# Layer 1's scan units ordered by pair of states instead of by channel group

## The chip, the core and the metric

The kernel runs on one core of a Trainium2 chip. The metric is the device time of one launch in microseconds. A core has several engines, each with an in-order queue of its own: TensorE (PE in the profile; PEld is its weight load), VectorE (DVE), ScalarE (ACT), GpSimd (POOL) and SyncE (SP, which here only issues DMAs). They share SBUF, 128 partitions of on-chip memory; PSUM, which TensorE writes its products to, is a second one; layer 1 lays it out as two tiles of 128 x 1024 f32 and four banks of 128 x 512. GpSimd does not touch PSUM in this kernel. An engine waits for another through semaphores, which a framework sets wherever one instruction needs what another wrote, or wants to overwrite what another still reads.

## What is computed

Two layers on an image of 64 x 64 positions with 96 channels. Each is a group norm, then a selective state-space scan, then a residual sum. The change lies in layer 1 alone, which scans the 4096 positions in one direction with 192 inner channels and 16 states:

```python
xz = jnp.einsum('blc,ec->ble', u, W_in)
xs, z = jnp.split(xz, 2, axis=-1)
xc = jax.nn.silu(causal_conv3(xs) + conv_b)
dbc = jnp.einsum('bld,ed->ble', xc, W_x)          # dt (6), B (16), C (16)
delta = jax.nn.softplus(jnp.einsum('blr,dr->bld', dt, W_dt) + b_dt)
dA = jnp.exp(delta[..., None] * A)
dBu = delta[..., None] * Bm[:, :, None, :] * xc[..., None]
def step(h, inp):
    dA_t, dBu_t, C_t = inp
    h = dA_t * h + dBu_t
    y = jnp.einsum('bdn,bn->bd', h, C_t)
    return (h, y)
...
y = (y + xc * D) * jax.nn.silu(z)
return jnp.einsum('bld,cd->blc', y, W_out)
```

(`causal_conv3` stands here for the sum over three shifted copies.) There are 192 x 16 scans over 4096 positions.

## The kernel before

The positions are cut into four **chunks** of 1024. The 192 channels form three **groups** of 64, and the 16 states eight **pairs** (n, n + 8). A **unit** is one group with one pair: 64 channels x 2 states fill the 128 partitions, 1024 positions lie along the free axis. A chunk has 24 units, the layer 96. Before the change unit i of a chunk is group i // 8 with pair i % 8, so eight units of a group run one after the other.

What one unit s needs, with the functions of class `Layer1`:

- `decay(s)`: ScalarE computes dA = exp(A dt), where dt is the group's row block, doubled onto both halves of the partitions (the **dup** tiles, made by `front_dup` with SP's DMAs, once for each group and chunk, for dt and for w = dt times u).
- B spread over the partitions. For most units `spread(s)` lets TensorE do it: a product of a 0/1 matrix (`pick`) with B, where B has been split into three bf16 parts that sum to its f32 value (`front_b`: ScalarE rounds, GpSimd subtracts). It lands in a PSUM tile `f`, and VectorE multiplies it by w in place (first half of `scan`). For the 20 units listed in `POOL_UNITS`, `load` fetches B from DRAM by DMA into a tile `B`, GpSimd multiplies it by w (`pool_f`), and dA goes to a PSUM tile `f`. Units 0 to 3 of the layer (`WHOLE`) take B unsplit in f32.
- `scan(s)`: VectorE's TENSOR_TENSOR_SCAN gives h from dA, w B and the last column of the chunk before. `keep_last` lets ScalarE keep that column.
- `times_c(s)`: GpSimd multiplies C by h, in place in the tile `C`, which `load(s)` has fetched by DMA, two DMAs of 256 KB for every unit.
- `fold(s)`, three units later (`LAG`): TensorE sums the two halves and the pairs into the group's PSUM bank `y0`, `y1` or `y2`, after `skip` has put D times u there. When a group's eight units are folded, `gate` multiplies by silu(z) on VectorE, into a tile `v`, and `back` makes the output of the chunk.

The `f` tiles come from one ring of two PSUM tiles of 128 x 1024; `y0`, `y1`, `y2` and `misc` hold one bank each. All other products of a chunk (convolution, projections, dt, z, output) go through `misc`, one at a time, with an eviction by ScalarE behind each.

The order is written out by hand. `Ordered` (from line 373; its `call` records every instruction, so that the profile gives line 389 for nearly all of layer 1) chains the instructions of each engine in the order in which the program names them. `run` goes through the units s; in each step it takes one piece of the generator `between` (the next chunk's projections and convolution, the output of the chunk before), then loads, spread, decays, one piece of `soft` (the next chunk's softplus: ScalarE's functions, two VectorE steps in `soft_vector`, w on GpSimd), the scan of unit s, C times h of unit s - 1, the fold of unit s - 3, and `hold`, products with a zero matrix that only keep TensorE at work. `start` prepares chunk 0 before the first unit: convolution, projections, and the softplus of the first two thirds of its columns (groups 0 and 1; dt and u hold 1536 columns, 512 in each part, and part 2 is group 2's). `end` closes the last chunk.

Of the kernel before, what the change touches and what calls it, by code (L numbers as in the profile page):

```python
# [39 lines left out]
WHOLE = 4  # L40

# [3 lines left out]
POOL_UNITS = ((5, 11, 15, 19, 23), (4, 8, 12, 16, 21), (4, 8, 12, 16, 21), (4, 8, 12, 16, 20))  # L45
# [1236 lines left out]
class Layer1:  # L1282
# [6 lines left out]
    def __init__(self, nc, tc, st, k, lay, w_in, conv_w, x1, stats, bc_dram, out, g):  # L1289
# [4 lines left out]
            for n, b in (  # L1294
                ("fix", 1), ("xn", 2), ("uz", 2), ("sp", 1), ("dt", 2), ("dup", 2), ("dbl", 1),
                ("parts", 2), ("split", 1), ("B", 1), ("C", 4 + LAG), ("dA", 3), ("h", 3), ("v", 1), ("oc", 1),
                ("ob", 2),
# [53 lines left out]
    def steps(self, matmuls):  # L1351

        for i, (args, kw) in enumerate(matmuls):
            self.nc.tensor.matmul(*args, **kw)
            if i % 2 or i == len(matmuls) - 1:
                yield
# [45 lines left out]
    def front_u(self, c):  # L1402
        of, self.at = self.chunks[c], c
        of["u"] = u = self.tile("uz", [P, CW], "u")
        for q in range(3):
            ps = self.misc(c, [P, NB], f"pc{q}")
            yield from self.steps(self.product(ps, q, self.conv_taps(of["xn"])))
            self.nc.scalar.activation(
                u[:, self.part(q)], ps, AF.Identity, bias=self.vec(CB, q)
            )  # L1410
# [27 lines left out]

    def front_dbl(self, c):
# [3 lines left out]
        for hf in range(2):  # L1443
# [3 lines left out]
            self.write_bc(c, hf)  # L1447

# [10 lines left out]
    def front_w(self, c, cols, engine):  # L1459
        of = self.chunks[c]  # L1460
        if "w" not in of:
            self.at = c
            of["w"] = self.tile("dt", [P, CW], "w")
        for col in cols:
            engine.tensor_mul(of["w"][:, col], of["dt"][:, col], of["u"][:, col])

    def front_dup(self, c, g, parts=(slice(0, CH),)):
# [4 lines left out]
        if not dup:  # L1472
            for name in ("dt", "w"):
                dup[name] = self.tile("dup", [P, CH], f"{name}1")
# [12 lines left out]
    def of_unit(self, name, s):  # L1487
        c, i = divmod(s, UNIT)
        return self.chunks[c]["dup"][i // PAIRS][name]

    def front_b(self, c, halves=False):

        nc, of = self.nc, self.chunks[c]
        dbl = of["dbl"]
        self.at = c
        of["B"] = parts = self.tile("parts", [B_ROWS, CH], "parts", BF16)
        rest = self.tile("split", [B_ROWS, CH], "rest")
        mid = self.tile("split", [B_ROWS, CH], "mid", BF16)
        copy = nc.gpsimd.tensor_copy if halves else nc.scalar.copy
        for col in (self.part(0), self.part(1)) if halves else (slice(0, CH),):  # L1500
            nc.scalar.copy(parts[:, col], dbl[0:B_ROWS, col])
            if not halves:
                yield
            nc.gpsimd.tensor_sub(rest[:, col], dbl[0:B_ROWS, col], parts[:, col])
            if not halves:
                yield
            copy(mid[64:96, col], rest[64:96, col])
            copy(parts[32:64, col], rest[32:64, col])
            if not halves:
                yield  # L1510
            nc.gpsimd.tensor_sub(parts[64:96, col], rest[64:96, col], mid[64:96, col])
            yield


    def on_pool(self, s):


        c, i = divmod(s, UNIT)
        return c < NSC and i in POOL_UNITS[c]

    def load(self, s):
        self.at, of = s, self.units[s]
        c, i = divmod(s, UNIT)
        for part, name in enumerate("BC"):
            if part or self.on_pool(s):
                of[name] = self.tile(name, [P, CH], name)
                load_states(
                    self.nc, of[name], self.bc_dram[part], 0, UNITS[1][i % PAIRS], c
                )

    def decay(self, s):
        self.at = s
        i = s % UNIT
        pool = "f" if self.on_pool(s) else "dA"
        self.units[s]["dA"] = da = self.tile(pool, [P, CH], pool)
        self.nc.scalar.activation(
# [3 lines left out]
    def spread(self, s):  # L1540
        self.at = s
        c, i = divmod(s, UNIT)
        self.units[s]["f"] = f = self.tile("f", [P, CH], "f")
        for hf in range(2):
            if s < WHOLE:
                pick, of = self.k["first"][:, i, :], "dbl"
            else:
                pick, of = self.k["pick"][:, i % PAIRS, :], "B"
            self.nc.tensor.matmul(
                f[:, self.part(hf)], pick, self.chunks[c][of][0:B_ROWS, self.part(hf)],  # L1550
# [3 lines left out]
    def scan(self, s):  # L1554
        self.at, of = s, self.units[s]
        c, i = divmod(s, UNIT)
        if not self.on_pool(s):
            self.nc.vector.tensor_mul(of["f"], of["f"], self.of_unit("w", s))
        of["h"] = self.tile("h", [P, CH], "h")
        self.nc.vector.tensor_tensor_scan(  # L1560
            of["h"], of["dA"], of["f"], self.last[:, i : i + 1] if c else 0.0, ALU.mult, ALU.add
# [7 lines left out]
    def keep_last(self, s):  # L1569
        i = s % UNIT  # L1570
        self.nc.scalar.copy(self.last[:, i : i + 1], self.units[s]["h"][:, CH - 1 : CH])

    def times_c(self, s):
        of = self.units[s]
        self.nc.gpsimd.tensor_mul(of["C"], of["C"], of["h"])
# [16 lines left out]
    def skips(self, c):  # L1592
        for g in range(1, GROUPS):
            self.skip(c, g)

    def fold(self, s):
        nc, k, terms = self.nc, self.k, self.units[s]["C"]
        c, i = divmod(s, UNIT)
        g, n = divmod(i, PAIRS)
        if i == 0:  # L1600
# [7 lines left out]

# [450 lines left out]
```

## Time and profile before

| | us |
|---|---|
| three runs | 576.94, 579.02, 594.4; median 579.02 |
| profiled execution, its own time | 575.46 |
| its span | 573.6 |
| layer 0 and the start of layer 1, to the first unit's multiply on VectorE | 189.9 |
| the 96 units, to the end of the last scan | 367.7 |
| from there to the end of the span | 16.0 |

Busy time in the span: TensorE 488.0 us, VectorE 469.2, GpSimd 345.8, ScalarE 329.2. In the stretch from 200 to 560 us it is about 309, 331, 299 and 202 of 360 us, added up from the busy time in windows.

How to read the profile: rows name an instruction as output<-inputs by the tiles' names, with partitions x elements, the number of such instructions, their busy time and the mean duration of one in ns, then the idle time of the engine just before them and what ended most of it. The timeline has start, duration, engine and instruction, and in brackets the idle time before it and what released it. A group's eight units run in a cadence of one multiply and one scan each on VectorE, or one scan alone where GpSimd does the multiply. PEclk is the clock that TensorE was granted; over the execution its mean is 0.897. SPq is the DMA queue that SP issues to.

### The profile page before, as it was taken

How to read it: one execution, taken by the hardware profiler on the slowest of the kernel's cores; microseconds unless marked ns; L12 is line 12 of the kernel's file. 1: busy time of each engine (PE TensorE's matmuls, PEld its weight loads, DVE VectorE, ACT ScalarE, POOL GpSimd, SP SyncE). 2: the span in 40 equal slices, each digit the busy share in tenths (PEclk: the TensorE clock that was granted, in tenths of full speed). 3: DMA queues.
4: the chain of work that ended last, by engine and by line, in shares of the span. 5: the costliest groups of instructions: out<-in, count | busy, mean ns of one | idle time of the engine just before them, and what ended most of it. 6: DMA issues, size and time to landing. Idle time of an engine off the chain costs nothing.

```text
span 573.6 us, 5312 instructions
## 1 busy us (share of the span) xinstructions
PE 488.0 (85%) x1493; PEld 168.3 (29%) x1493; DVE 469.2 (82%) x447; ACT 329.2 (57%) x486; POOL 345.8 (60%) x206
## 2 busy tenths in 40 slices
PE   4999899988899596987798988979958768989794
PEld 3544354447632221221222222212212111222121
DVE  6897989248614599989989979999979989899981
ACT  5448993479454695677575684664584545243300
POOL 7080000015210496968987978788877888797960
PEclk9999999999997697988989978969987775997998
DMA  5103800000006954895989994997995897999901
GB/s 169 25 9 82 269 2 0 0 1 1 24 4 157 237 152 123 196 236 128 212 200 247 225 226 125 236 215 182 231 233 150 207 207 186 231 229 230 233 19 34
DMA packets 35241, 84.24 MB, mean 147 GB/s; under 512 B 13313, under 2 KB 14589, under 8 KB 34947
## 3 DMA queue, kind: packets, MB, share of 16 engines
q1 hardware_dynamic: 33922, 82.29, 60.1%
q10 hardware_dynamic: 1280, 1.52, 0.8%
q8 instruction: 14, 0.23, 0.2%
q14 instruction: 25, 0.20, 0.1%
HBM read 68.99 MB, written 2.25 MB: 124 GB/s over the span
## 4 chain that ended last, share of the span: by engine, by line
PE 34%; DVE 27%; ACT 18%; DMA 8%; POOL 5%; issue 4%; SPq 3%; DVEq 0%; POOLq 0%; ACTq 0%
DVE h L389 17%; PE y L389 8%; PE pc L389 7%; DVE f L389 5%; ACT q L389 3%; DMA C<-bc_dram 3%; PE f L389 3%; SPq L389 3%; ACT L389 3%; PE po L389 3%; DMA B<-bc_dram 2%; ACT f L389 2%; PE pz L389 2%; PE pw L389 2%; DMA dt<-dt 2%
## 5 line engine op out<-in xcount | busy, mean ns | idle before, releaser
L389 POOL TENSOR_TENSOR C<-C,h 128x1024 f32<-128x1024 f32 x96 | 227.7, 2388 | 36.9 <-DVE h L389 17.1
L389 DVE TENSOR_TENSOR_SCAN h<-dA,last,f 128x1024 f32<-128x1024 f32 x57 | 133.8, 2347 | 8.4 <-POOL C L389 0.7
L389 PE MATMUL y<-C,both 128*64 128x512 f32 x384 | 120.6, 714 | 1.9 <-POOL C L389 1.9
L389 DVE TENSOR_TENSOR f<-f,w 128x1024 f32<-128x1024 f32 x76 | 92.2, 1213 | 17.4 <-PE f L389 11.8
L389 ACT ACTIVATE dA<-dt,A 128x1024 f32<-128x1024 f32 x76 | 86.3, 1142 | 4.3 <-DMA dt<-dt 2.7
L389 PE MATMUL f<-parts,pick 96*128 96x512 bf16 x144 | 50.6, 438 | 26.2 <-DVE h L389 23.4
L389 PE MATMUL pc<-pad,cw 96*128 96x512 f32 (+1 forms) x144 | 57.3, 555 | 3.3 <-ACT v L389 3.3
L389 POOL TENSOR_TENSOR B<-B,w 128x1024 f32<-128x1024 f32 x20 | 47.6, 2378 | 19.8 <-DMA B<-bc_dram 6.1
L389 ACT COPY last<-h 128x1 f32<-128x1 f32 x72 | 13.5, 188 | 71.8 <-DVE h L389 71.8
L389 PE MATMUL y<-within,zeros 128*128 128x512 f32 x82 | 48.6, 693 | 0.0
L389 DVE TENSOR_TENSOR_SCAN h<-dA,f 128x1024 f32<-128x1024 f32 x19 | 43.5, 2287 | 2.4
L389 PE MATMUL pc<-xn,cw 96*64 96x512 f32 (+1 forms) x84 | 34.4, 679 | 12.4 <-ACT dt L389 6.5
L389 ACT ACTIVATE f<-dt,A 128x1024 f32<-128x1024 f32 x20 | 22.3, 1115 | 34.7 <-DVE h L389 26.2
L389 ACT ACT_TABLE_LOAD x28 | 35.9, 1283 | 8.6 <-DMA dt<-dt 6.5
L389 PEld LDWEIGHTS y<-C,both 128*64 128x64 f32 x384 | 22.1, 149 | 56.3 <-issue 42.5
L389 PEld LDWEIGHTS pc<-pad,cw 96*128 96x128 f32 x144 | 26.9, 189 | 33.3 <-issue 25.8
L389 DVE TENSOR_TENSOR_SCAN h<-f,last,B 128x1024 f32<-128x1024 f32 x15 | 34.9, 2329 | 1.4 <-POOL B L389 1.4
L389 PEld LDWEIGHTS <-pick 96*128 96x128 bf16 x144 | 10.3, 102 | 87.4 <-DVE h L389 50.5
L389 POOL TENSOR_TENSOR rest<-dbl,parts 96x1024 f32<-96x1024 f32 (+1 forms) x5 | 8.7, 1744 | 32.5 <-ACT parts L389 32.4
L389 POOL TENSOR_SCALAR ln_small<-ln_small 128x4 f32<-128x4 f32 x2 | 0.5, 235 | 42.5 <-DVE ln_small L389 42.5
L389 PEld LDWEIGHTS y<-within,zeros 128*128 128x128 f32 x82 | 14.3, 209 | 36.5 <-issue 36.5
L389 POOL MEMSET wda<- 128x4 f32 (+3 forms) x8 | 1.0, 119 | 37.5 <-ACT wda L389 37.5
(214 smaller groups left out, 736.1 us busy)
## 6 DMA issues: line engine op xcount, KB each, us to landing
C<-bc_dram SPq DMA_DIRECT2D x192, 256.0 KB, 5.2
B<-bc_dram SPq DMA_DIRECT2D x40, 256.0 KB, 4.7
dt<-dt SPq DMA_DIRECT2D x14, 256.0 KB, 4.8
w<-w SPq DMA_DIRECT2D x14, 256.0 KB, 7.6
dt<-dt SPq DMA_DIRECT2D x20, 128.0 KB, 4.7
w<-w SPq DMA_DIRECT2D x20, 128.0 KB, 5.3
wB<-rows_dram SPq DMA_DIRECT2D x1, 1472.0 KB
wC<-rows_dram SPq DMA_DIRECT2D x1, 1472.0 KB
```

Source lines behind the costliest of these rows:

```text
L389: ins = it(*args, **kw)
```

## The change

Unit i of a chunk is now pair i // 3 with group i % 3, so three units in a row share B and C.

- B is spread once for three units (`spread(s)` where s % 3 is 0), into `self.b`. The second and third unit (and unit 0 of the layer) multiply it by w into another `f` tile, `self.f`, which both use. The first unit of every three has its w B from GpSimd: 31 units instead of 20.
- C is loaded once for three units, B once for each that GpSimd multiplies. h tiles are 16 columns longer, the scan writes them from column 16 on, and `times_c` writes its product into the same tile from column 0 on, so that C stays.
- The split of B into bf16 parts is done by TensorE and ScalarE: ScalarE rounds from PSUM, and `less` lets TensorE subtract what has been rounded, by a product of the f32 rows with the identity and one of the bf16 parts with -1 entries (`k["less"]`).
- All three groups' dup tiles must be there from a chunk's first units on. In `start` the softplus of the third part is done with the other two, and the first part of chunk 1's convolution is made there as well. The dup tiles of groups 0 and 1 are filled in turn, part by part.
- The gates of a chunk come in the first steps of the next one, in place in `sz`; those of the last chunk come after the last scan. `hold`'s places change (37 of them, before 41), and so do the buffers of the tile pools.

The core of the diff:

```diff
-                ("fix", 1), ("xn", 2), ("uz", 2), ("sp", 1), ("dt", 2), ("dup", 2), ("dbl", 1),
-                ("parts", 2), ("split", 1), ("B", 1), ("C", 4 + LAG), ("dA", 3), ("h", 3), ("v", 1), ("oc", 1),
-                ("ob", 2),
+                ("fix", 1), ("xn", 2), ("uz", 2), ("sp", 1), ("dt", 1), ("dup", 2), ("dbl", 1),
+                ("parts", 2), ("B", 2), ("C", 3), ("dA", 3), ("h", 3 + LAG), ("oc", 1), ("ob", 2),
...
+    def less(self, i, c, hf, ps):
+        of, col = self.chunks[c], self.part(hf)
+        self.nc.tensor.matmul(
+            ps, self.k["ident"][0:B_ROWS, 0:B_ROWS], of["dbl"][0:B_ROWS, col],
+            start=True, stop=False,
+        )
+        self.nc.tensor.matmul(ps, self.k["less"][:, i, :], of["B"][:, col], start=False, stop=True)
+
+    def split(self, c, hf, ps, bank):
+        of, col = self.chunks[c], self.part(hf)
+        if "B" not in of:
+            self.at = c
+            of["B"] = self.tile("parts", [B_ROWS, CH], "parts", BF16)
+        for i, rows in enumerate((slice(0, B_ROWS), slice(0, 64), slice(32, 64))):
+            self.nc.scalar.copy(of["B"][rows, col], ps[rows, :])
+            if i < 2:
+                ps = bank(f"less{i}_{hf}")
+                yield lambda ps=ps, i=i: self.less(i, c, hf, ps)
...
     def on_pool(self, s):
-        c, i = divmod(s, UNIT)
-        return c < NSC and i in POOL_UNITS[c]
+        return s % GROUPS == 0 and 0 < s < NSC * UNIT
...
     def scan(self, s):
         if not self.on_pool(s):
-            self.nc.vector.tensor_mul(of["f"], of["f"], self.of_unit("w", s))
-        of["h"] = self.tile("h", [P, CH], "h")
+            if i % GROUPS == (1 if s > GROUPS else 0):
+                self.f = self.tile("f", [P, CH], "f")
+            of["f"] = self.f
+            self.nc.vector.tensor_mul(of["f"], self.b, self.of_unit("w", s))
+        of["h"] = self.tile("h", [P, CH + SHIFT], "h")
         self.nc.vector.tensor_tensor_scan(
-            of["h"], of["dA"], of["f"], self.last[:, i : i + 1] if c else 0.0, ALU.mult, ALU.add
+            of["h"][:, SHIFT:], of["dA"], of["f"], self.last[:, i : i + 1] if c else 0.0,
+            ALU.mult, ALU.add,
         )
...
     def times_c(self, s):
-        of = self.units[s]
-        self.nc.gpsimd.tensor_mul(of["C"], of["C"], of["h"])
+        h = self.units[s]["h"]
+        self.nc.gpsimd.tensor_mul(h[:, 0:CH], h[:, SHIFT:], self.units[s - s % GROUPS]["C"])
...
     def start(self):
...
-        for p in range(2):
+        pc1 = bank("y2", [P, NB], "pc1")
+        do(self.product(pc1, 0, self.conv_taps(self.chunks[1]["xn"])))
+        self.at = 1
+        self.chunks[1]["u"] = self.tile("uz", [P, CW], "u")
+        for p in range(3):
             col = self.part(p)
             nc.scalar.activation(sq[:, col], pv[p], AF.Abs, bias=self.vec(DTB, p))
             soft_scalar(nc, self.k, sq[:, col], acc[:, col], sq[:, col])
             nc.vector.tensor_scalar(dt[:, col], pv[p], self.vec(DTB, p), 0.0, ALU.add, ALU.max)
-        for s in range(3):
-            self.load(s)
-        for p in range(2):
+        self.load(1, 0)
+        self.load(0, 3)
+        self.load(1, 3)
+        for p in range(3):
             col = self.part(p)
             soft_vector(nc, dt[:, col], acc[:, col], sq[:, col])
-            self.front_w(0, (col,), nc.vector)
-            self.front_dup(0, 0, (col,))
+            self.front_w(0, col, nc.vector)
+            if p < 2:
+                for g in range(2):
+                    self.front_dup(0, g, (col,))
+        self.front_dup(0, 2)
         self.spread(0)
-        self.spread(1)
+        for s in range(2):
+            self.decay(s)
+        nc.scalar.activation(
+            self.chunks[1]["u"][:, self.part(0)], pc1, AF.Identity, bias=self.vec(CB, 0)
+        )
+        parts = [
+            self.split(0, hf, pd[hf], lambda name, y=f"y{hf}": bank(y, [B_ROWS, NB], name))
+            for hf in range(2)
+        ]
+        for _ in range(3):
+            for later in [next(part, None) for part in parts]:
+                if later:
+                    later()
         pz = [bank(f"y{g}", [P, NB], f"pz{g}") for g in range(GROUPS)]
         for g in range(GROUPS):
             do(self.z_product(pz[g], g, xn))
-        for s in range(2):
-            self.decay(s)
-        nc.scalar.activation(dt[:, self.part(2)], pv[2], AF.Identity, bias=self.vec(DTB, 2))
-        for _ in self.front_b(0, halves=True):
-            pass
...
     def run(self):
...
-            if 1 <= s < WHOLE:
-                self.spread(s + 1)
+            self.late = None
+            if 0 < c and 1 <= i <= GROUPS:
+                self.gate(c - 1, i - 1)
+            if s % GROUPS == 0 and 0 < s < n:
+                self.spread(s)
             if s < n:
                 next(work, None)
-            if s + 3 < n:
-                self.load(s + 3)
-            if WHOLE <= s < n - 1 and not self.on_pool(s + 1):
-                self.spread(s + 1)
+            if s % GROUPS == 1:
+                self.load(0, s + 5)
+            if s % GROUPS == 2:
+                self.load(1, s + 4)
             if 0 < s <= n - UNIT:
                 self.keep_last(s - 1)
-            if self.on_pool(s + 1):
-                self.decay(s + 1)
-                self.pool_f(s + 1)
             if s + 2 < n and not self.on_pool(s + 2):
                 self.decay(s + 2)
             if s < n:
                 next(soft, None)
                 self.scan(s)
+            if self.on_pool(s + 1):
+                self.decay(s + 1)
             if 1 <= s <= n:
                 self.times_c(s - 1)
-            if s == n:
+            if self.on_pool(s + 2):
+                self.pool_f(s + 2)
+            if s > n:
                 next(end)
             if s >= LAG:
                 self.fold(s - LAG)
+            if self.late:
+                self.late()
             if s < n:
                 self.hold(s)
-            if i in (20, 21) and c < NSC:
-                self.gate(c, i - 20)
```

## The prediction

> I call the parts of one unit **M** (VectorE's w times B), **S** (its scan), **T** (GpSimd's C times h), **F** (GpSimd's w times B, where it takes M's place) and **spread** (the TensorE product that fills PSUM with B); M(s), S(s) are those of unit s. Three units that share a pair of states are a trio.
>
> **What bounds the kernel now.** I read the page's busy shares first. They say little: TensorE 85%, VectorE 82%, over stages with different limits. Layer 1 holds the change, and there I read the waits of VectorE from 205 us to the end:
>
> ```profile
> DVE f L389 <- PE f L389: 9.0, 6, 3.3
> DVE v L389 <- PE y L389: 5.6, 1, 5.6
> DVE h L389 <- POOL B L389: 3.7, 2, 2.3
> DVE acc L389 <- ACT q L389: 3.0, 1, 3.0
> ```
>
> The columns are total wait, times, longest. In some 350 us VectorE waits under 25 us: it sets layer 1's pace. The rows that load it and GpSimd:
>
> ```profile
> L389 POOL TENSOR_TENSOR C<-C,h 128x1024 f32<-128x1024 f32 x96 | 227.7, 2388 | 36.9 <-DVE h L389 17.1
> L389 DVE TENSOR_TENSOR_SCAN h<-dA,last,f 128x1024 f32<-128x1024 f32 x57 | 133.8, 2347 | 8.4 <-POOL C L389 0.7
> ...
> L389 DVE TENSOR_TENSOR f<-f,w 128x1024 f32<-128x1024 f32 x76 | 92.2, 1213 | 17.4 <-PE f L389 11.8
> ...
> L389 POOL TENSOR_TENSOR B<-B,w 128x1024 f32<-128x1024 f32 x20 | 47.6, 2378 | 19.8 <-DMA B<-bc_dram 6.1
> ```
>
> VectorE's timeline gives the cadence: start to start, as the durations overlap.
>
> ```profile
> 314.00 1.21 DVE L389 TENSOR_TENSOR f<-f,w 128x1024 f32<-128x1024 f32 x1
> 315.35 2.35 DVE L389 TENSOR_TENSOR_SCAN h<-dA,last,f 128x1024 f32<-128x1024 f32 x1
> 317.61 2.32 DVE L389 TENSOR_TENSOR_SCAN h<-f,last,B 128x1024 f32<-128x1024 f32 x1
> 319.85 1.21 DVE L389 TENSOR_TENSOR f<-f,w 128x1024 f32<-128x1024 f32 x1
> ```
>
> M to S takes 1.34 us, S to the next 2.26: a unit with M costs 3.60 (3.54 in chunk 0), one with F 2.24 (2.20). M(0) starts at 189.89, S(2) at 201.09, S(95) ends at 557.62, and 16.0 us follow to the span's 573.6. From S(2) on VectorE takes 356.5 us; the single waits that I read there (2.29 and 1.39 for F, 2.25, 3.28, 2.06 and shorter ones for the spread, 3.00 for ScalarE) add to 16.9.
>
> [...] the softplus step on 512 columns takes 0.69 us at 180 us with GpSimd idle, 2.92 us at 212.56 beside a GpSimd product. [...] S's follower starts 0.09 us before S's end when it doesn't wait for it, and in layer 0, where it does,
>
> ```profile
> 86.67 6.29 DVE L389 TENSOR_TENSOR_SCAN wB<-wda,wg 128x2944 f32<-128x2944 f32 x1
> 93.00 3.23 DVE L389 TENSOR_TENSOR wg<-wB,wC 128x2944 f32<-128x2944 f32 x1
> ```
>
> 0.04 us after it: 0.13 us for such a wait. [...] after 6.5 us idle, four passes took 3.78 us at 192.86, against 1.88 at 202.13.
>
> **The change, part by part**, against the profiled 575.46 us (0.6% under the 579.02 median).
>
> *VectorE's stretch from S(2) on.* M stays for the second and third of each trio and for unit 0: 65 instead of 76. Eleven units go from 3.6 to 2.24: 11 x 1.35 = **-14.9**. The third part of chunk 0's softplus moves to the start: 212.56 to 218.18 in the timeline, **-5.6**. Two of the last chunk's gates fall behind S(95): 2 x 0.58 = **-1.2**. The other three softplus pairs took 6.4, 5.5 and 5.5 us beside GpSimd; I take 5.3, as GpSimd then has only one T to do before it waits for them: **-1.5** (0 to -3).
> *A new wait on VectorE itself.* M now writes a bank other than B's. M(3k+1) writes where the dA that S(3k) reads lay, M(3k+2) where S(3k+1) has just read its input, so each waits for the scan in front of it: 64 x 0.13 = **+8** (0 if that price doesn't hold here, which is the other end).
> *The waits.* The 16.9 us go or change. F's input is loaded two trios ahead and T's loads fall from 96 to 32, so the 3.7 us behind DMAs go. What is late next is the ring of two PSUM banks. Spread(3k) waits for S(3k-1), and M(3k+1) wants it 2.24 us later; a spread takes 0.61 us, or 1.04 at half clock, but behind it on TensorE's queue are front products, folds, the split's products and holds, which must be through by the next spread. dA(3k+3) waits for M(3k+2), and on ScalarE it stands behind dA(3k+4): 0.19 + 1.15 + 1.12 of 3.6 us, 0.9 to spare. I put 10 us here: 2.6 after the start (below), 2 for ScalarE, 5.4 for TensorE at half clock, near the 9.0 of before: **-6.9** (-15 to +3). Sum of the stretch: **-22.1**.
>
> *The start*, which pays. Before:
>
> ```profile
> 179.23 0.75 DVE L389 TENSOR_SCALAR dt<-f_pv,vec 128x512 f32<-128x512 f32 x1 [2.84 <-ACT q L389]
> ...
> 183.84 1.19 SPq L389 DMA_DIRECT2D dt<-dt  x2
> ...
> 188.75 1.28 ACT L389 ACT_TABLE_LOAD   x1 [6.54 <-DMA dt<-dt]
> ```
>
> That TENSOR_SCALAR waits for ScalarE's absolute value of its part. There are now three ahead of the first softplus step, and the third part's comes on ScalarE at 178.53 + 3.68 + 0.67 = 182.9: the step starts at 183.75, not 179.89 (+3.9). Then SP: pairs of DMAs every 1.27 us. The dt that S(0) needs last was the third pair and is now the fifth, since group 1's first halves come in between (+2.5): landed 3.7 us after issue at 195.2, table load and decay to 197.6, where S(0) was at 191.23. Then ScalarE's order: decay(1) to 198.7, u 0.67, two copies of 0.58, then the split: four pairs of products, each with a copy behind it, then three gate products with their copies, and only then decay(2). A pair is two fp32 passes and a bf16 one: 0.85 x 2 + 0.4 = 2.1 at half clock, which TensorE has after some 13 us idle (since the first spread), 1.1 at full. From the first copy's end at 199.95, three pairs at half clock and one at full end at 207.5, the gates at 210.5, the copy at 211.2, decay(2) at 212.4. S(2) starts at 212.6, not 201.09: **+11.5** (+8 at full clock, +15 at half throughout; the DMAs of group 2 alone would give +4). On ScalarE u, two copies of the last column and decay(4) then precede decay(3): S(3) waits 1.8 us, S(6) 0.8, the 2.6 above.
>
> *The tail.* Three folds stood behind the end's products (560.38 to 563.2). Two of them now come before: **-1.8** (0 to -3).
>
> *No cost*: last-column copies and the other decays (as many as before); the split in later chunks (four ScalarE copies of 1.04 us and two GpSimd subtractions of 2.1 go, six copies of 0.58 come; ScalarE is 56% busy from 200 to 560 us); on SP the same dup DMAs and 106 fewer loads, of 256 KB each. GpSimd: 96 x 2.388 + 31 x 2.378 + 3 x 3.44 = 313 us, under VectorE's; a trio is 4 x 2.33 = 9.3 against VectorE's 2 x 3.60 + 2.24 + 0.26 = 9.7. That cover is thin: rival 2.
>
> Sum: -22.1 + 11.5 - 1.8 = -12.4: **563 us**, 2.8% under the median, 2.1% under the profiled run. I leave the 0.6% between them out.
>
> **The rivals.**
> 1. *The start is cheap and the new wait free.* TensorE at full clock: -3.5; no 0.13: -8; few TensorE waits: -3. It gives **549**. [...] Against: the layer 0 pair above.
> 2. *GpSimd becomes the pace.* If T in place within h costs 2.5 rather than 2.33, a trio is 9.9 and VectorE waits for F, and softplus and gates no longer find GpSimd ahead: some 0.3 us a trio, 10 us: **573**. For: 0.4 us of room. Against: the form of T is as before, and F has 1.2 us in hand behind the softplus.
> 3. *TensorE becomes the bound: slower than before.* From 200 to 560 us it is busy 309 of 360. Now 44 spreads of 0.70 go, 4 holds of 1.19, and 12 split pairs of 1.55 come: about 290 of 344, as full as before, with a wait for VectorE at the head of each trio. The clock was half in about 28% of that time, so 290 us are 290 x 0.86 = 250 at full clock, 7.8 a trio; at that clock 7.8 / 0.86 = 9.1, against 10.6 for VectorE with softplus and gates. It becomes the bound when half clock reaches 53%, eats the whole 12.4 us at 58%, and at 67%, where a trio takes 11.7, 1.1 x 32 = 36 us are added: **599**. For: idle at each head. [...]
>
> **The numbers.** Forecast 0.52, rivals 0.20, 0.16, 0.12. About 2% (11.6 us, 567.4 to 590.6) is what a measurement tells from no change. The forecast's own range (waits 5 to 17, start +8 to +15) is 553 to 574: four fifths of it are faster. Faster: 0.42 + 0.20 = 0.62; within: 0.10 + 0.14 = 0.24; slower: 0.14, with rival 2's end. The range 547 to 580 leaves out rival 3 and the ends.
>
> **What would show it.** VectorE's rows: 65 M, 96 S, as long as before. S to M start to start 2.39 instead of 2.26 (2.26: no wait). S(2) near 212, with ScalarE's decay behind the gate copies. T at 2.39. Waits for F near zero. S(95)'s end near 547. Wrong if S(2) starts before 208 or after 217, if VectorE's waits after it exceed 20 us, or if GpSimd has no idle time left.

## The result and the profile after

The changed kernel is slower: 593.42 us (median of 4 runs, 592.27 to 594.66) against 577.98 us (4 runs beside it, 576.46 to 594.4), a ratio of 1.0277 with a 95% interval of 1.0236 to 1.0317. The forecast was 563. Some runs of a kernel come out over 1.5% longer than its fastest (before, 594.4 and 576.46 us); times and ratios in the experiments below leave those out. The profiled execution took 594.66 us, span 592.9; TensorE's mean clock is 0.848, before 0.897.

| profiled, us | before | forecast | after | difference |
|---|---|---|---|---|
| layer 0, to the second TENSOR_SCALAR of the start | 179.23 | | 184.51 | +5.3 |
| from there to S(2) | 21.9 | +11.5 | 29.75 | +7.9 |
| S(2) to the end of S(95) | 356.5 | -22.1 | 361.65 | +5.1 |
| tail | 16.0 | -1.8 | 17.0 | +1.0 |

The waits of VectorE from 205 us to the end, the view that opened the prediction:

```profile
DVE h L387 <- ACT f L387: 22.7, 9, 6.3
DVE f L387 <- PE f L387: 13.7, 6, 6.4
DVE sz L387 <- PE y L387: 5.8, 5, 2.2
DVE h L387 <- ACT dA L387: 5.7, 1, 5.7
```

The first row is new: nine scans waited for a dA in PSUM (`f`) from ScalarE, one of them 6.3 us. The work itself is as forecast; these are the rows that answer to those shown of before:

```profile
L387 POOL TENSOR_TENSOR h<-h,C 128x1024 f32<-128x1024 f32 x96 | 233.2, 2437 | 93.1 <-DVE h L387 47.6
...
L387 DVE TENSOR_TENSOR_SCAN h<-dA,last,f 128x1024 f32<-128x1024 f32 x48 | 112.6, 2346 | 3.4
L387 DVE TENSOR_TENSOR f<-f,w 128x1024 f32<-128x1024 f32 x65 | 80.0, 1231 | 22.0 <-PE f L387 13.7
...
L387 POOL TENSOR_TENSOR B<-B,w 128x1024 f32<-128x1024 f32 x31 | 73.0, 2356 | 0.0
```

65 multiplies of the old length, 96 C products of 2.44 us in place, 31 w B on GpSimd that nobody waits for. And VectorE's timeline of one trio (start, duration):

```profile
386.38 1.23 DVE L387 TENSOR_TENSOR f<-f,w 128x1024 f32<-128x1024 f32 x1
387.65 2.35 DVE L387 TENSOR_TENSOR_SCAN h<-dA,last,f 128x1024 f32<-128x1024 f32 x1
390.03 1.23 DVE L387 TENSOR_TENSOR f<-f,w 128x1024 f32<-128x1024 f32 x1
391.37 2.35 DVE L387 TENSOR_TENSOR_SCAN h<-dA,last,f 128x1024 f32<-128x1024 f32 x1
393.63 2.32 DVE L387 TENSOR_TENSOR_SCAN h<-f,last,B 128x1024 f32<-128x1024 f32 x1
```

S to the M behind it takes 2.38 us where the M waits for that S, S to S 2.26. So what grew is waits. In the stretch from S(2) to S(95) they add to 38.9 us (S(2)'s own not counted), forecast 10; without them the stretch is 322.7 us, forecast 324.4.

**Where a wait comes from.** The longest for a dA is at S(36), the longest for the spread at M(61). Each stands in or right behind a stretch of half clock, 327 to 344 and 422.5 to 446.5 us. TensorE's timeline in the first, and ScalarE's beside it:

```profile
337.87 5.49 PE L387 MATMUL pc<-xn,cw 96*128 96x512 f32 x6
343.29 1.46 PE L387 MATMUL y<-h,both 128*64 128x512 f32 x4
344.68 2.84 PE L387 MATMUL pc<-xn,cw 96*128 96x512 f32 x6
```

```profile
343.40 0.69 ACT L387 ACTIVATE u<-pc,vec 128x512 f32<-128x512 f32 x1 [5.50 <-PE pc L387]
...
346.49 1.10 ACT L387 ACTIVATE f<-dt,A 128x1024 f32<-128x1024 f32 x1
```

The same convolution product takes 5.49 us at half clock and 2.84 at full. ScalarE's eviction of it waited 5.50 us, dA of the next trio's first unit stood behind the eviction, and S(36) started at 347.68 after 6.25 us of waiting. The windows view of the second stretch (busy time of TensorE, its weight load, VectorE, ScalarE and GpSimd, then the granted clock, the DMA engines' share and GB/s):

```profile
422.50:446.50 24.00, 24.00 (x46) 5.04 (x42) 16.47 (x10) 13.42 (x18) 19.22 (x9) 0.50 0.24 57
```

Of the 365 us from 210 to 575, TensorE had half clock for 140 us (sum over windows of 5 us); before 99 us (the 142 and 93 of the expectations are the same, read more roughly). What it waited for at a trio's head had grown too:

```profile
PE f L387 <- DVE h L387: 35.6, 16, 6.9
```

23.4 us before. So the theories tested were: **clock** (TensorE idles at each trio's head, where the spread waits for S(3k-1), gets half clock, and is then late for everyone), **ScalarE's order** (dA stands behind evictions that wait for TensorE), **TensorE's load** (the split's products make it too full), and **places in PSUM** (dA's tile comes free too late, VectorE waits for itself).

The first of them leaves something out. In the window from 210 to 575 us, TensorE was idle for no more of the time than before (365 us less its busy time, the first number behind the 365: 60.7 us before, 53.1 after, of which half clock itself, by longer products, has filled some):

```profile
210.00:575.00 365.00, 304.34 (x871) 74.63 (x870) 323.33 (x185) 194.32 (x252) 289.09 (x123) 0.86 0.80 189
```

```profile
210.00:575.00 365.00, 311.92 (x816) 80.30 (x812) 314.11 (x171) 199.50 (x270) 304.72 (x127) 0.81 0.47 115
```

And the two long stretches do not begin behind a head. Of the 140 us at half clock, 58.0 lie in stretches whose longest idle time, in the 3.4 us ahead of them (as long as the shortest such stretch in that record), was a spread waiting for a scan (34.1 of 99 before). But 54.6 lie in three stretches, at 245, 327 and 422.6 us, with only 0.72 us of idle time ahead, between the last product of the split and the first dt product (`pv`), which waited for ScalarE's copy of `parts`:

```profile
419.06 1.10 PE L387 MATMUL less<-dbl,ident 96*96 96x512 f32 x2
420.00 0.38 PE L387 MATMUL less<-parts,less 96*96 96x512 bf16 x1
421.10 1.12 PE L387 MATMUL pv<-dbl,dtw 6*128 6x512 f32 x2 [0.72 <-ACT parts L387]
422.15 1.57 PE L387 MATMUL y<-h,both 128*64 128x512 f32 x4
423.65 2.07 PE L387 MATMUL pv<-dbl,dtw 6*128 6x512 f32 x2
```

So a wait at a head stood ahead of a part of the added half clock, and none stood in the 3.4 us ahead of these three stretches.

### The profile page after: what moved, and what is told of

It is laid out like the page before. It is cut to its first block, busy times and chain, and to the rows that moved or that the text cites. A ratio compares the mean times of both kernels' runs of the same rounds, so it can differ in the third digit from the quotient of the medians.

```text
span 592.9 us, 4899 instructions
## 1 busy us (share of the span) xinstructions
PE 498.3 (84%) x1439; PEld 174.8 (29%) x1439; DVE 458.1 (77%) x441; ACT 328.4 (55%) x496; POOL 354.4 (60%) x203
## 4 chain that ended last, share of the span: by engine, by line
PE 46%; DVE 20%; ACT 18%; DMA 6%; SPq 4%; issue 4%; POOL 1%; DVEq 0%; ACTq 0%; POOLq 0%
PE y L387 12%; DVE h L387 10%; PE pc L387 9%; PE po L387 7%; DVE f L387 4%; SPq L387 4%; DMA C<-bc_dram 3%; ACT q L387 3%; DMA dt<-dt 2%; ACT L387 2%; PE pw L387 2%; ACT f L387 2%; ACT dA L387 2%; PE pz L387 2%; ACT wg L387 2%
## 5 line engine op out<-in xcount | busy, mean ns | idle before, releaser
L387 POOL TENSOR_TENSOR h<-h,C 128x1024 f32<-128x1024 f32 x96 | 233.2, 2437 | 93.1 <-DVE h L387 47.6
L387 PE MATMUL y<-h,both 128*64 128x512 f32 x384 | 124.4, 739 | 0.1
L387 DVE TENSOR_TENSOR_SCAN h<-dA,last,f 128x1024 f32<-128x1024 f32 x48 | 112.6, 2346 | 3.4
L387 DVE TENSOR_TENSOR f<-f,w 128x1024 f32<-128x1024 f32 x65 | 80.0, 1231 | 22.0 <-PE f L387 13.7
L387 POOL TENSOR_TENSOR B<-B,w 128x1024 f32<-128x1024 f32 x31 | 73.0, 2356 | 0.0
L387 DVE TENSOR_TENSOR_SCAN h<-f,last,B 128x1024 f32<-128x1024 f32 x24 | 56.0, 2334 | 17.3 <-ACT f L387 15.6
L387 PE MATMUL f<-parts,pick 96*128 96x512 bf16 x62 | 22.4, 448 | 35.6 <-DVE h L387 35.6
L387 ACT ACTIVATE f<-dt,A 128x1024 f32<-128x1024 f32 x31 | 34.4, 1110 | 28.0 <-DVE f L387 27.7
L387 PEld LDWEIGHTS y<-h,both 128*64 128x64 f32 x384 | 24.8, 156 | 77.3 <-issue 52.0
L387 DVE TENSOR_TENSOR_SCAN h<-dA,f 128x1024 f32<-128x1024 f32 x17 | 38.9, 2287 | 6.9 <-ACT dA L387 5.7
L387 PE MATMUL po<-sz,w_out 64*96 64x512 f32 x42 | 30.1, 836 | 0.0
L387 ACT COPY last<-h 128x1 f32<-128x1 f32 x72 | 13.2, 187 | 21.9 <-DVE h L387 21.6
L387 POOL MEMSET wda<- 128x4 f32 (+3 forms) x8 | 1.0, 119 | 37.5 <-ACT wda L387 37.5
```

The source lines that it names most:

```text
L387: ins = it(*args, **kw)
```

## The experiments

Times are medians; ratios are those on record against the kernel before in the same round, and where a kernel has few runs they differ from the quotient of the medians. The medians of the kernel before were 577.4 us in the round of e1 to e4, 577.9 in that of e5 to e7, 579.4 in that of e8 to e10, and 572.3 (two runs) beside e11. The last three columns are of the profiled run: the stretch from S(2) to S(95), the waits in it, the rest.

| | us | ratio (95%) | stretch | waits | rest |
|---|---|---|---|---|---|
| before | | 1 | 356.5 | 16.9 | 339.6 |
| changed | 593.4 | 1.028 (1.024 to 1.032) | 361.7 | 38.9 | 322.7 |
| e1 ScalarE's order | 601.2 | 1.038 (1.030 to 1.045) | 375.3 | 54.3 | 321.0 |
| e2 PSUM roles | 582.0 | 1.013 (1.003 to 1.023) | 349.0 | 30.2 | 318.8 |
| e3 15 holds | 580.8 | 1.005 (1.003 to 1.008) | 351.0 | 28.3 | 322.7 |
| e4 no split on TensorE | 582.2 | 1.007 (1.003 to 1.011) | 359.4 | 36.7 | 322.7 |
| e5 = e2 + e3 | 580.9 | 1.006 (1.003 to 1.009) | 352.1 | 33.2 | 318.9 |
| e6 = e5 + e1 | 606.2 | 1.049 (1.042 to 1.056) | 374.2 | 57.2 | 317.0 |
| e7 = e5 + start | 576.6 | 0.998 (0.995 to 1.001) | 350.1 | 31.1 | 319.0 |
| e8 product ahead of spread | 575.8 | 0.987 (0.979 to 0.996) | 346.1 | 23.5 | 322.6 |
| e9 = e8 + e3 | 578.1 | 0.995 (0.992 to 0.998) | 353.7 | 31.4 | 322.3 |
| e10 = e9 + e2 + start | 573.5 | 0.983 (0.977 to 0.989) | 349.0 | 30.8 | 318.2 |
| e11 = e10 without holds | 574.0 | 0.987 (0.973 to 1.000) | 350.7 | 32.3 | 318.4 |

The last column is 321 to 323 us wherever the order of VectorE's work is that of the change, and some 4 us less with e2's roles (6 in e6): the table is one about waits.

**e1.** In `run`, for s = 3k+2, the multiply and both decays come ahead of the step's evictions. The edit does more than its expectation says: `next(work)` moves in every step, so all its evictions now stand behind `keep_last` too, which waits for the scan in front, and in the steps 3k behind `decay(s + 2)`.

```diff
-            if s < n:
-                next(work, None)
...
+            early = s < n and self.on_pool(s + 1)
+            if early:
+                self.multiply(s)
+                self.decay(s + 1)
             if s < n:
+                next(work, None)
                 next(soft, None)
```

> Edit: in the last unit of each trio, s = 3k+2, ScalarE's decays (dA of 3k+4 and 3k+3) are put ahead of the evictions and softplus steps of that step; the order of TensorE is as it was. If the waits come from ScalarE's order (dA of 3k+3 stands behind evictions that wait for a late TensorE product), VectorE's waits for ScalarE at a scan, 22.7 us in the changed kernel, fall below 10, and the time falls from 593.4 by 10 to 15 us to about 580. If the cause is TensorE's clock or its load, the evictions only come later and TensorE with them: the time stays within 5 us of 593 (588 to 598), and VectorE's waits for TensorE (13.7 us at the multiplies) stay or grow by some 5.

VectorE's waits for ScalarE fell to 3.6 us, as the order theory had it, but those for TensorE at the multiplies rose from 13.7 to 43.1, and the time by 8, more than either case had. ScalarE's order isn't the cause by itself: the evictions free `misc`, TensorE's next product waits for that (TensorE's waits for ScalarE rose from 17.2 to 47.3 us between 210 and 575 us), and behind the product stands the next spread. Both ends of ScalarE's queue are tight. TensorE's waits at the heads were only 18.2 us here, half of those after the change, and its half-clock time was still 130 us: once more, waits at the heads alone don't make it.

**e2.** The ring of two PSUM tiles becomes two tiles with fixed roles:

```diff
-        for n, b in (("f", 2), ("y0", 1), ("y1", 1), ("y2", 1), ("misc", 1)):
+        for n, b in (("fa", 1), ("fb", 1), ("y0", 1), ("y1", 1), ("y2", 1), ("misc", 1)):
...
-        pool = "f" if self.on_pool(s) else "dA"
+        pool = "fa" if self.on_pool(s) else "dA"
...
-                self.f = self.tile("f", [P, CH], "f")
-            of["f"] = self.f
+                self.f = self.tile("fa", [P, CH], "fa")
+            of["f"] = self.b if i % GROUPS == 2 else self.f
```

(`self.b` is in "fb".)

> Edit: the two PSUM tiles get fixed roles, one for dA of the trio's first unit and the output of the second unit's multiply, one for B, in which the third unit multiplies in place. 32 waits of VectorE for its own scan go (32 x 0.13 = 4.2 us), and dA of 3k+3 has its place free after the scan of 3k+1, not after the multiply of 3k+2, 3.6 us earlier. If a late place for dA is what makes ScalarE late, the waits for ScalarE at a scan halve as well (22.7 to about 11) and the time is about 577 to 582. If it is not, only the own waits go: about 589, and the scan of 3k+1 starts its multiply 2.26 us after (no wait) where it was 2.38. If the own waits cost nothing either, 593.

The rest fell by 3.9 us: 32 own waits of 0.12 us (S(3k+1) to M(3k+2), start to start, 2.26 us instead of 2.38). The scans still waited 17.4 us for ScalarE instead of 22.7, not 11, so dA's place was a small part; M(61) waited 6.43 us as before. The half-clock time was 105 us in this run, and the runs spread from 578.5 to 590.7, so it tells little that the median, 582.0, lies in the range of the first case.

**e3.**

```diff
+        if n == 0 and i > 4 and i % GROUPS == 2:
+            n = 1
         for _ in range(n):
```

> Edit: 15 more products with the zero matrix (1.19 us each at full clock, 18 us in all), at the end of the steps 3k+2, where TensorE then waits for the scan before the next spread. If the clock is the cause (TensorE idles at a trio's head, is halved, and is then late), the half-clock time in the records from 210 to 575 us falls from 142 towards the 93 us of the kernel before, VectorE's waits for TensorE at the multiplies fall from 13.7 to under 7 us, and the time is 575 to 585. If TensorE has too much to do (load, not clock), the added 18 us make these waits grow by 10 or more: 600 or above. If ScalarE's order alone matters: 593 within 4.

More work, less time: 580.8 us over 20 runs, 579.3 to 582.3. Half-clock time fell from 140 to 86 us. The window from 210 to 575 us:

```profile
210.00:575.00 365.00, 310.81 (x878) 84.59 (x874) 318.07 (x176) 198.78 (x270) 307.18 (x127) 0.88 0.48 115
```

TensorE is busy as long as after the change (310.81 against 311.92 us) with 15 products more, since they run faster. Both long stretches of half clock are gone (the dt products at 323.51 and 327.06 us took 1.12 and 1.07 us, after the change 2.07 and 1.97), and with them the two longest waits: S(36) waited 1.69 us, M(61) under 0.6. That shows the clock as a cause, and speaks against TensorE's load, which asked for 600 us. But VectorE still waited 8.4 us for TensorE (under 7 was expected) and 18.5 for ScalarE. Nor did the holds work where they were meant to: the stretches behind a head hardly shrank (58.0 to 51.2 us), and those behind the split's last product went from 54.6 to 3.4. Why these went is not shown.

**e4.** `split` and `less` give way to the `front_b` of before, with `rest` in a buffer of its own and one `ob` buffer less.

```diff
-            for self.late in self.split(c, hf, ps, bank):
+            for _ in range(2):
                 yield
...
+            if i in ((18, 20, 21, 22) if c == 0 else (14, 16, 18, 20)):
+                next(parts, None)
```

> Edit: B's split back to ScalarE and GpSimd as in the kernel before, with the order of units, the shared B and C and the rest as changed (one buffer less for the output tile). TensorE loses 12 to 16 pairs of products, some 19 us at full clock in layer 1's stretch, and GpSimd gets 6 subtractions of about 2.1 us in its place; at the start ScalarE and GpSimd make the four parts. If TensorE's load is the cause, VectorE's waits for TensorE and ScalarE after the first units fall by 10 or more and the time is 575 to 583. If the clock is the cause, less work means more idle time: half-clock time stays at 140 us or grows, and the time stays within 590 to 600. If the start's split alone matters, the scan of unit 2 starts 3 to 8 us earlier than at 214.3 and the rest is as it was: 586 to 590.

S(2) started 10.0 us after M(0), after the change 14.6, and S(3) 15.8 instead of 18.8: the start's split on TensorE costs 4.6 us there, of which 3.0 last. In the profiled run VectorE's waits for TensorE and ScalarE fell from 36.4 to 27.1 us, near the 10 that the load theory asked for, but new waits for GpSimd (6.4 us) took most of that back, and half clock was 146 us. That run took 587.45 us; the median, 582.2, lies within what the load theory expected, and the clock of these runs (0.836 to 0.861) was no better than the 0.847 to 0.850 after the change. So taking the split off TensorE gained 11 us without a better clock. The start explains a part; the rest was not profiled, and that the split's products cost something in the trios as well stays open.

**e5, e6, e7.** Combinations; the start's edit of e7 is

```diff
         self.spread(0)
+        idle = self.misc(0, [P, NB], "idle")
+        for _ in range(10):
+            nc.tensor.matmul(
+                idle, self.k["zero"], free(self.k["within"], (1, NB)), start=True, stop=True
+            )
...
-        for _ in range(3):
+        for i in range(3):
             for later in [next(part, None) for part in parts]:
                 if later:
                     later()
+            if i == 1:
+                self.decay(2)
```

with `decay(2)` left out of step 0.

> Edits: the fixed roles of the two PSUM tiles (as in e2) and the 15 added holds (as in e3). If the two act on different waits (holds on TensorE's clock; roles on VectorE's own waits and on when dA's place is free), they add up against e3's 580.8: own waits -4.2, and the scans' waits for ScalarE from 18.5 towards e2's 17 or below, so 573 to 577. If the gain of e2 came only from a luckier clock in its runs (they spread from 578 to 591), e5 stays at 579 to 581.

> Edits: e5 and ScalarE's order of e1 (decays ahead of the evictions in the step 3k+2). In e1 dA of 3k+3 had to wait for the multiply of 3k+2, and the evictions behind it on ScalarE stood with it; with the fixed roles its place is free after the scan of 3k+1. If that wait made e1 slow, the order now helps: scans' waits for ScalarE after the first units below 6 us, TensorE's below 12, and the time is 563 to 569. If evictions that come 2.3 us later are by themselves what makes TensorE late, VectorE's waits for TensorE grow to 25 us or more and the time is 580 or above.

> Edits: e5, and in the start two things: 10 products with the zero matrix (12 us at full clock) behind the first spread, where TensorE otherwise idles 16.6 us ahead of the split's first product, and dA of unit 2 on ScalarE ahead of the split's last copies and of the three gate copies. If the start's cost is the half clock there and the place of dA of unit 2, as the prediction worked out, the first products of the split take 1.1 us and not 2.0, the scan of unit 2 starts at 206 to 208 instead of 212.6, and the time is e5's less 4 to 7. If the DMAs of group 2 set the start anyway (the last of them lands near 206), unit 2's scan comes no earlier than 210 and the time is e5's less 0 to 2.

e5 is e3 again, as its second case had it: the 4 us of own waits are gone from the rest and came back as waits. e6 is the slowest of all, with 46.5 us of waits for TensorE although its half-clock time was 109 us: its ScalarE order is bad even with a better place for dA and a better clock than after the change. In e7 S(2) came 9.8 us after M(0) instead of 14.8, but S(3) then waited:

```profile
206.95 2.29 DVE L387 TENSOR_TENSOR_SCAN h<-dA,fb 128x1024 f32<-128x1024 f32 x1 [0.90 <-ACT dA L387]
...
216.19 2.29 DVE L387 TENSOR_TENSOR_SCAN h<-fa,B 128x1024 f32<-128x1024 f32 x1 [6.95 <-ACT fa L387]
```

S(3) stands 19.0 us behind M(0), as in e5 (18.9): a gain given back within one unit. The split's first products still took 2.02 us; the added products had ended 5.3 us ahead of them. Yet its median is 4 us below e5's, with a clock of 0.91 instead of 0.89. In the profiled runs the gain lies behind S(3): from there to the end of S(95) 340.8 us, in e5 348.0, with half clock for 75 instead of 92 us. Why the clock was better there, these runs don't tell.

**e8.** Two statements of `run` change places, nothing is added:

```diff
-            if s % GROUPS == 0 and 0 < s < n:
-                self.spread(s)
             if s < n:
                 next(work, None)
+            if s % GROUPS == 0 and 0 < s < n:
+                self.spread(s)
```

> Edit on the changed kernel alone: at a trio's head TensorE does the product of the next chunk's (or output's) piece first and the spread behind it, so that it has work while it waits for the scan of 3k-1; no work is added. If idle time at the heads is what halves the clock, TensorE's waits of the spread for the scan fall from 36 to under 20 us, half-clock time from 210 to 575 us from 142 to about 100, and the time is 577 to 586 (as with the 15 added holds). If the cause is that TensorE has too much to do, the spread comes later still, VectorE's waits for TensorE at the multiplies grow from 13.7 to 25 us or more, and the time is 595 to 610.

A swap of two statements took 17.6 us off the median (the changed kernel was measured in an earlier round), and the ratio went from 1.028 to 0.987 (0.979 to 0.996); by the medians, 575.8 and 579.4, the lead on the kernel before is 0.6%, so its size is open. Half-clock time fell to 94 us, as expected; TensorE's waits at the heads only to 30.6 us, not under 20. Of the half clock, 37.5 us lie behind a head and 23.9 behind the split. What the swap does beside the clock is seen at the last chunk's first output products. TensorE after the change:

```profile
519.05 1.03 PE L387 MATMUL f<-parts,pick 96*128 96x512 bf16 x2 [2.89 <-DVE h L387]
519.88 1.91 PE L387 MATMUL po<-x,ident 96*96 96x512 f32 x2
521.72 2.02 PE L387 MATMUL po<-sz,w_out 64*96 64x512 f32 x2
```

and in e8:

```profile
508.87 1.02 PE L387 MATMUL po<-x,ident 96*96 96x512 f32 x2
509.82 1.10 PE L387 MATMUL po<-sz,w_out 64*96 64x512 f32 x2
511.93 0.60 PE L387 MATMUL f<-parts,pick 96*128 96x512 bf16 x2 [1.01 <-DVE h L387]
```

The products needed nothing of the scan, but stood behind a spread that waited 2.89 us for it; then they ran at half clock. In the gap they run at full clock and are done ahead of the spread. ScalarE, changed kernel first, then e8:

```profile
531.34 0.58 ACT L387 COPY oc<-po 96x512 f32<-96x512 f32 x1 [12.52 <-PE po L387]
```

```profile
516.52 0.58 ACT L387 COPY oc<-po 96x512 f32<-96x512 f32 x1 [4.81 <-PE po L387]
```

The scan that waited 5.40 us behind that copy (S(84)) no longer waits, and VectorE's waits for ScalarE from 205 us on:

```profile
DVE f L387 <- PE f L387: 11.4, 6, 4.2
DVE h L387 <- ACT f L387: 10.0, 5, 2.7
```

In e3, with 86 us of half clock, the second row was 18.5, so the clock alone does not bring it down. The spread at the head costs in two ways: the product behind it is late, and with it its eviction and the dA behind that; and stretches of half clock follow on some of its waits (58.0 us of them after the change, 37.5 in e8). How the 17.6 us divide between the two, e8 can't tell, as it changes both.

**e9, e10, e11.** e10's start edit is e7's `decay(2)`, and `decay(3)` right behind the scan of unit 1, ahead of that step's piece of `between`:

```diff
+            if s == 1:
+                self.decay(3)
+                next(work, None)
-            if self.on_pool(s + 1):
+            if s > 2 and self.on_pool(s + 1):
                 self.decay(s + 1)
```

> Edits: e8 and the 15 added holds of e3. If both act by the clock alone, and e3 left half-clock episodes behind idle heads (2.9 us at 506 us, 4.1 at 466, 6.9 at 486), these go too: 568 to 576, with a clock of 0.91 or more. If the hold, the product and the spread then stand in one row between two scans (1.2 + 2.2 + 0.6 us at full clock, twice that at half, for 3.6 us from the scan of 3k-1 to the multiply of 3k+1), the spread is late at most heads: VectorE's waits for TensorE above 25 us and 585 or more.

> Edits: the fixed roles of the PSUM tiles, the 15 holds, the product ahead of the spread, and in the start dA of unit 2 ahead of the split's last copies and dA of unit 3 right behind the scan of unit 1, ahead of the evictions of the first pieces. In e7 unit 2's scan came 6 us earlier, and unit 3's then waited 6.95 us for its dA; here it should wait for GpSimd's w B at most: the scan of unit 3 starts at 213 (16 us after the first multiply) and not 19. Then e9 less 3 to 6 us: 564 to 572 if e9 is at 570. If in the start the split's products or unit 3's w B set the pace anyway, unit 3's scan is still 18 to 19 us behind the first multiply and the time is e9's.

> Edit: e10 without the 15 added holds (fixed roles of the PSUM tiles, product ahead of the spread, and the start's two decays). With the product in the gap the holds are only load: e9 with them took 579.7, e8 without 575.9. If so, VectorE's waits for TensorE at the multiplies fall from e10's 20 us to about 10 and the time from 573.5 to 567 to 571. If the holds still pay by the clock, half-clock time grows and the time is 574 to 580.

Three expectations were missed. e9 fell between its two cases (VectorE's waits for TensorE 20.4 us, half clock 97 us). e10 took 573.5 us, 564 to 572 were expected. e11 did not reach 567 to 571: at 574.0 us, with half clock for 99 us where e10 had 78 (in a profiled run of 579.24 us, its longest), it lies in the case in which the holds still pay, but it isn't told apart from e10. So with the product in the gap the holds bring no gain that these runs show (e9 against e8, e11 against e10: the intervals overlap). In e10 S(3) starts 15.0 us after M(0), not 18.8: the start's 3.7 us. At 573.5 us, 1.7% under the kernel before (1.1 to 2.3), it has the lowest median of these, though not told apart from e8 and e11.

**e12.** The kernel before once more, unchanged.

> The kernel before, unchanged, for a second profile of it. Layer 0 and the first part of the start have the same instructions in both kernels, but the second TENSOR_SCALAR of the start begins at 179.23 us in the one profile of before and at 180.9 to 184.5 in the profiles of the changed kernel and of the experiments. If that is TensorE's clock in layer 0, which differs from run to run, it begins anywhere from 179 to 185 here, and later the more half-clock time layer 0 has. If the change lengthens layer 0, it begins at 179.2 again, within 0.5.

Its second TENSOR_SCALAR began at 181.96 us, 2.7 us later than in the first profile, with 18.8 us of half clock in the first 180 us instead of 8.1. So a layer 0 of other length needs no change in the program, and 2.7 of the +5.3 us of the table above are within what two profiles of one kernel differ by. The other 2.6 stay open: the changed kernel and the experiments began it at 180.9 to 187.1 us, and not strictly later with more half clock. (The time, 574.78, was one run.)

## Why the prediction was wrong

**The work on VectorE: right.** 11 M fewer, the softplus part and two gates moved out, and 64 waits of an M for the scan in front at 0.13 us: without the other waits 324.4 us were forecast, 322.7 measured. S to M start to start is 2.38 us (2.39 forecast). e2 takes half of these waits away and the rest falls by 3.9 us, so rival 1's free wait doesn't hold.

**The waits: this is the step that failed.** "I put 10 us here: 2.6 after the start (below), 2 for ScalarE, 5.4 for TensorE at half clock, near the 9.0 of before". Measured: 38.9, of which 22.7 for ScalarE, 13.7 for TensorE, 1.6 for a DMA and 0.9 for gates. These 29 us too many are the miss: the sum came to -12.4, the medians differ by +15.4, 28 us apart. Two things were wrong in the term:
- The half clock of before was taken over. Its share went from 27% to 38%; e3 and e8 bring it back to 23 and 26%, and most or all of the time with it. A part of it stands behind the heads (58.0 us of half clock, before 34.1). Another 54.6 us began where the split's last product meets the dt products, and the split in later chunks had been put under "no cost". Whether the split makes these stretches stays open: e4, without it, had half clock for 146 us.
- For ScalarE only its own durations were added ("0.19 + 1.15 + 1.12 of 3.6 us, 0.9 to spare"). The list of what stands behind the spread on TensorE's queue was made, but the chain was not followed on: product, eviction, dA, scan. e8 shows it by moving the product.

**Rival 3** was the nearest, in its time (599) and in naming TensorE late behind the heads, but its threshold (53% half clock) came from averages for a trio. 38% was enough. The single waits shown above (6.25 and 6.43 us, each at the end of a long stretch) suggest why: a mean lets one trio's slack pay for another's lateness. And a TensorE that was late and busy stayed at half clock: from 422.5 to 446.5 us it was busy for 24.00 of 24.00 us, at a granted clock of 0.50.

**The start: right in kind, too large.** +11.5 forecast, +8 to +15 as bounds; +7.9 measured without layer 0's share, just under the lower bound. S(2) waited 5.73 us for its dA behind the gate copies, as worked out. But counted from the second TENSOR_SCALAR, S(0) came 1.9 us earlier than forecast, and from there to S(2) it took 13.3 us, not 15.0: only two of the four pairs ran at half clock, not three. S(2)'s place at 214.3, in the range that was named for it, owes something to luck, as layer 0 took 5.3 us more in this profile.

**The tail: right in kind.** Its two folds moved (in e2 and e8 the tail is 14.3 and 14.5 us, -1.6), but after the change the last folds ran at half clock, behind 2.88 us of idle time at 566 us: 17.0.

**Rival 2** fell: C times h did get longer (2.44 us, near its 2.5), but GpSimd's C products waited 47.6 us for scans, and no scan waited for w B.

## What to carry to other kernels

When a change lets an in-order queue wait at a new place, follow everything behind the waiting instruction to its end, over the other queues too, and put what doesn't need the awaited data ahead of it: here that was two statements and 17.6 us. A forecast can't take TensorE's clock over from the profile before just because its idle time stays the same: here that time did not grow (60.7 us before, 53.1 after), and half clock went from 99 to 140 us. More could be read from what stood right ahead of each stretch of half clock: behind a head lay 34.1 us of it before, and 58.0 after. Where an engine's work sum is sure to 2 us and its waits are a guess, the range has to come from the waits.

## What was not expected of the hardware

In the clock's record of the changed kernel, the stretches of half clock in layer 1 last 3.4, 6.8, 10.2, 13.7, 17.1 and 23.9 us, multiples of 3.4. In the two at 327 and 422.6 us TensorE was busy 17.0 of 17.0 and 24.00 of 24.00 us, and stayed at half clock to their end. (The profile models the ends of products, so "busy" here means no more than that a product was under way by its account.)

Nor was there always idle time where the full clock was lost: in e4 the records show no gap on TensorE from 405.4 to 418.5 us, and half clock began at 417.0:

```profile
413.63 1.12 PE L387 MATMUL pv<-dbl,dtw 6*128 6x512 f32 x2
414.68 1.08 PE L387 MATMUL y<-h,both 128*64 128x512 f32 x4
415.69 1.12 PE L387 MATMUL pv<-dbl,dtw 6*128 6x512 f32 x2
416.74 1.77 PE L387 MATMUL y<-h,both 128*64 128x512 f32 x4
```

These are dt products (`6*128` in the record) and folds (`128*64`), as at the three stretches of the changed kernel. But such products did not always lose the full clock. The sequence shown above at 419 us kept the full clock in e8, with the same gap:

```profile
416.65 1.10 PE L387 MATMUL less<-dbl,ident 96*96 96x512 f32 x2
417.59 0.38 PE L387 MATMUL less<-parts,less 96*96 96x512 bf16 x1
418.69 1.12 PE L387 MATMUL pv<-dbl,dtw 6*128 6x512 f32 x2 [0.72 <-ACT parts L387]
419.74 1.08 PE L387 MATMUL y<-h,both 128*64 128x512 f32 x4
420.75 1.12 PE L387 MATMUL pv<-dbl,dtw 6*128 6x512 f32 x2
```

What decided between the two is not shown: no run varied the timing of such a sequence by itself, nor the kind of product.
